# How a routed layer brings its rows to its experts: written to places and read back, or fetched by a list

## The chip, the cores and the metric

The kernel runs on one core of one Trainium2 chip. The metric is device time in microseconds (us), the median of several executions. A second number is the span: the time from the first to the last instruction in an execution that the hardware profiler recorded. Five engines work in parallel on the core, each on its own queue in order: PE (TensorE, matmuls; PEld is its weight load), DVE (VectorE), ACT (ScalarE), POOL (GpSimd) and SP (which issues DMA transfers). They wait for each other through semaphores.

## The reference

Eight layers run one after the other on 625 nodes of 512 features, each adding to `x`: four graph layers and four feed-forward layers. The change lies in the first feed-forward layer, `L0_ffn`: attention over the 625 nodes, a layernorm, and then a routed layer in which each node goes through one of eight experts. Cut to what matters:

```python
t = h.reshape(b * s, d)                       # 625 x 512, after attention and layernorm
probs = softmax(t @ gate_W + gate_b)          # 625 x 8
idx = argmax(probs); gw = max(probs)
hid = gelu(einsum('nd,edf->enf', t, W1) + b1) # eight experts, 512 -> 2048
out_all = einsum('enf,efd->end', hid, W2) + b2
out = einsum('ne,end->nd', one_hot(idx, 8), out_all) * gw[:, None]
```

The output depends only on the chosen expert of each node, so the kernel computes each expert for its own nodes alone.

## The kernel before

The nodes lie as five tiles of 125 rows (`NT = 5`, `P = 125`), the features as four blocks of 128 (`KC = 4`). Each expert has room for 128 nodes (`SLOTS = 128`), so there are 8 x 128 = 1024 places. A node that finds its expert full gets a place beyond these, and a slower path, `L0_late`, computes it; that path runs only if a count, `most`, is over 128, which all engines test at the end of the layer (L891, L892). The trace shows none of its instructions.

The order of the work in `L0_ffn`:

1. SP loads the first six tiles of expert weights, 1 MB each (`ring`, six buffers, L676). It then writes zeros to the 1024 places of `places` (L719) and to part of `made` (L722), both in device memory.
2. Projections and attention; the layernorm of line L164 and L165 leaves the rows in `t_tok`, in the core's memory.
3. The router: `t_tok` transposed (L173), logits `pg` (L230, a helper's line), softmax, the largest of eight, and `oh`, its one-hot.
4. The rank of a node among those of its expert comes from products with a triangle of ones (`before`, L778) and with ones (L779). Expert times 128 plus rank is the node's place: `slot` in f32, `to` as an integer (L791).
5. The rows travel. Five indirect DMAs on POOL (L793) write the 125 rows of each node tile to the places in `places`; eight DMAs on SP (L797) read 128 rows for each expert into `at_e`. All five write the same tensor, and the framework lets each wait for the one before.
6. Meanwhile DVE and PE turn `slot` into a row over all partitions (`srow`, L809 to L812) and make `gt`, the one-hot of the last expert (L828).
7. PE transposes the rows of each expert (L817), DVE and ACT copy them by turns to `xg`.
8. Experts: for each of 8 x 4 steps `first` (16 matmuls, L837), GELU on ACT (L842) and `second` (4 matmuls, L851), one step apart. The rows of experts 0 to 6 go to `made` (L860). In the last expert five indirect DMAs fetch each node's result from `made` (`take`, L866); DVE adds them to `x` (L871). The last expert's own results reach the nodes by a product with `gt` (L875, L889).

A planner decides the order on each engine from dependences and from when a tile's memory comes free. So tiles that are allocated later in the program can be loaded early: the tiles `wx` and `bsel` of the recurrent layer (L1286, L1308) are loaded on ACT's queue at about 519 us, in the middle of `L0_ffn`, and scaled on DVE (L1288, L1309).

Of the kernel before, what the change touches and what calls it, by code (L numbers as in the profile page):

```python
# [15 lines left out]
F32 = mybir.dt.float32  # L16
F16 = mybir.dt.float16
BF16 = mybir.dt.bfloat16
I32 = mybir.dt.int32
U32 = mybir.dt.uint32  # L20
U16 = mybir.dt.uint16
AF = mybir.ActivationFunctionType
ALU = mybir.AluOpType
AX = mybir.AxisListType
# [4 lines left out]
N, D, P, NT = 625, 512, 125, 5  # L29
# [11 lines left out]
SLOTS = 128  # L41
# [608 lines left out]
def L0_ffn(C):  # L650
# [5 lines left out]
    nc, tc, I = C.nc, C.tc, C.ins  # L656
    E8, FF = 8, 2048
# [4 lines left out]
    with ExitStack() as st:  # L662
# [7 lines left out]
        def load(upto):  # L670

            for key in parts[len(loaded):upto]:
# [3 lines left out]
                nc.sync.dma_start(w, src.rearrange("(k p) n -> p k n", p=128))  # L676
                loaded[key] = w


        places = C.dram.tile([E8 * SLOTS + N, D], F32, name="places")  # L680
        made = C.dram.tile([E8 * SLOTS + N, D], F32, name="made")
        zero = pool.tile([128, D], F32, name="zero")
        nc.gpsimd.memset(zero, 0.0)
# [2 lines left out]
        t_tok = pool.tile([P, NT, D], F32, name="t_tok")  # L686
        with ExitStack() as st2:
            apool = st2.enter_context(tc.tile_pool(name="aa", bufs=1))
            qT = apool.tile([128, KC, N], F32, name="qT")
            kT = apool.tile([128, KC, N], F32, name="kT")  # L690
            v = apool.tile([P, NT, D], F32, name="v")
            with tc.tile_pool(name="a_ps", bufs=2, space=PSUM) as ps:
                xT = apool.tile([128, KC, N], F32, name="xT")
                C.feature_major(ps, xT, xn)
                bo = C.row_bcast(pool, W("bo"), D, "bias", 2)
                for t in range(NT):
                    nc.gpsimd.tensor_add(xn[:, t], xn[:, t], bo[:P])
                for dst, w, b in ((qT, "Wq", "bq"), (kT, "Wk", "bk")):
                    wt = C.weight(W(w).rearrange("(k p) n -> p k n", p=128), KC)
                    col = C.columns(pool, ps, W(b).rearrange("(c p) -> c p", p=128), KC, "col_" + b)  # L700
                    for c in range(KC):
                        for n0, n in HALVES:
                            pq = ps.tile([128, 512], F32, name="pq")
                            C.linear_T(pq[:, :n], xT, n0, n, wt, c)
                            nc.scalar.activation(dst[:, c, n0:n0 + n], pq[:, :n], AF.Identity,
                                                 bias=col[:, c:c + 1])
                wt = C.weight(W("Wv").rearrange("(k p) n -> p k n", p=128), KC)
                bv = C.row_bcast(pool, W("bv"), D, "bias", 2)
                for t in range(NT):
                    pv = ps.tile([P, D], F32, name="pv")  # L710
                    C.linear(pv, xT, t, wt)
                    nc.vector.tensor_add(v[:, t], pv, bv[:P])
            wt = C.weight(W("Wo").rearrange("(k p) n -> p k n", p=128), KC)
            g = C.row_bcast(pool, W("ln1_g"), D, "ln_g")
            b = C.row_bcast(pool, W("ln1_b"), D, "ln_b")
            st_ = C.small.tile([P, NT, 6], F32, name="ln_st")

            for e in range(E8):
                nc.sync.dma_start(places[e * SLOTS:(e + 1) * SLOTS], zero[:SLOTS])  # L719
            for r in range((E8 - 1) * SLOTS, E8 * SLOTS + N, 128):  # L720
                n = min(128, E8 * SLOTS + N - r)
                nc.sync.dma_start(made[r:r + n], zero[:n])  # L722

            def finish(t, out):
                for half in range(2):
                    part = xn[:, t, half * 256:(half + 1) * 256]
                    nc.vector.tensor_add(part, part, out[half])
                nc.vector.bn_stats(st_[:, t], xn[:, t])

            C.attention(qT, kT, v, wt, 1.0 / 8.0, False, finish)  # L730
            C.layernorm(t_tok, xn, g, b, st_)

        tT = pool.tile([128, KC, N], F32, name="tT")
        sel = pool.tile([P, NT, E8], F32, name="sel")
# [2 lines left out]
        with ExitStack() as st2:  # L737
            E2 = st2.enter_context
            rpool = E2(tc.tile_pool(name="a_r", bufs=1))
            R = lambda shape, name: rpool.tile(shape, F32, name=name)  # L740
            beyond = R([P, NT], "beyond")
            nc.gpsimd.iota(beyond, pattern=[[P, NT]], base=E8 * SLOTS, channel_multiplier=1,
                           allow_small_or_imprecise_dtypes=True)
            place = R([128, E8], "place")
            nc.gpsimd.iota(place, pattern=[[SLOTS, E8]], base=0, channel_multiplier=1,
                           allow_small_or_imprecise_dtypes=True)
            before = R([P, P], "before")
            nc.vector.tensor_scalar(before, C.iota[:P, :P], place[:P, 0:1], None, op0=ALU.is_gt)
            to = rpool.tile([P, NT], U32, name="to")
            xg = R([128, KC, E8 * SLOTS], "xg")  # L750
            srow = R([128, N], "srow")
            slot, rk, gv = R([P, NT], "slot"), R([P, NT], "rk"), R([P, NT], "gv")
            oh, rank, base = (R([P, NT, E8], k) for k in ("oh", "rank", "base"))
            with tc.tile_pool(name="a_ps3", bufs=2, space=PSUM) as ps, tc.tile_pool(name="a_at", bufs=1) as work:
# [35 lines left out]
                nc.vector.tensor_add(slot, slot, beyond)  # L790
                nc.vector.tensor_copy(to, slot)  # L791
                for t in range(NT):
                    nc.gpsimd.indirect_dma_start(out=places[:, :], in_=t_tok[:, t], in_offset=None,  # L793
                                                 out_offset=bass.IndirectOffsetOnAxis(ap=to[:, t:t + 1], axis=0))
                at_e = [work.tile([SLOTS, D], F32, name="at_e", bufs=E8) for e in range(E8)]
                for e in range(E8):
                    nc.sync.dma_start(at_e[e], places[e * SLOTS:(e + 1) * SLOTS])  # L797
                top = pool.tile([1, 1], F32, name="top")
                nc.vector.tensor_add(base[0:1, 0], base[0:1, NT - 1], pn[0:1, 1, NT - 1])
                nc.vector.reduce_max(top, base[0:1, 0], axis=AX.X)  # L800
# [944 lines left out]


PHASES = [graph_and_L0_gnn, L0_ffn, L1_gnn, L1_ffn, L2_gnn, L2_ffn, L3_gnn, L3_ffn]


# [48 lines left out]
```

## Time and profile before

| what | value |
|---|---|
| median of three runs | 5357.06 us (5355.81 to 5363.99) |
| the profiled execution, its own time | 5365.64 us |
| its span | 5363.8 us, 184920 instructions |
| mean granted TensorE clock | 0.966 |
| PE busy | 4975.2 us, 93% of the span |
| DVE, ACT, POOL busy | 2690.5, 1100.6 and 61.6 us |
| moved by DMA | 232.19 MB, mean 43 GB/s |

The costliest groups of instructions all belong to the recurrent layer, which takes most of the span in 625 steps:

```profile
L1496 PE MATMUL pa<-wp,left 128*23 128x384 bf16 x33312 | 1502.7, 327 | 129.7 <-issue 39.2 <-DVE left L1633 7.4
L1496 PEld LDWEIGHTS pa<-wp,left 128*23 128x23 bf16 x33312 | 811.0, 93 | 643.9 <-DVE left L1633 153.9 <-issue 108.8
```

Such a line gives the kernel's line, the engine and operation, output and inputs with their shapes, and the count; then the busy time in us, the mean duration of one in ns, and the idle time of the engine just before them with what ended it. The routed layer lies between about 455 and 750 us of the span. A timeline line has the start, the busy time, the engine, the line, the operation and its tiles; what stands in brackets is how long the engine had been idle before and what released it. Issuing a DMA isn't counted as busy time, except for indirect DMAs on POOL, which show as instructions[...].

### The profile page before, as it was taken

How to read it: one execution, taken by the hardware profiler on the slowest of the kernel's cores; microseconds unless marked ns; L12 is line 12 of the kernel's file. 1: busy time of each engine (PE TensorE's matmuls, PEld its weight loads, DVE VectorE, ACT ScalarE, POOL GpSimd, SP SyncE). 2: the span in 40 equal slices, each digit the busy share in tenths (PEclk: the TensorE clock that was granted, in tenths of full speed). 3: DMA queues.
4: the chain of work that ended last, by engine and by line, in shares of the span. 5: the costliest groups of instructions: out<-in, count | busy, mean ns of one | idle time of the engine just before them, and what ended most of it. 6: DMA issues, size and time to landing. Idle time of an engine off the chain costs nothing. (4 is left out here: it accounts for less than half of the span.)

```text
span 5363.8 us, 184920 instructions
## 1 busy us (share of the span) xinstructions
PE 4975.2 (93%) x74524; PEld 3140.2 (59%) x74524; DVE 2690.5 (50%) x13552; ACT 1100.6 (21%) x4478; POOL 61.6 (1%) x57
## 2 busy tenths in 40 slices
PE   7986999999999979999999999999999999999988
PEld 5555755555556645555555555565555655555545
DVE  6533024240025146666666656666566666656258
ACT  7433111110115111111111111111111111111125
POOL 0000000000000000000000000000000000000000
PEclk9987998989989989999999999999999999999988
DMA  1031962221116310000000000000000000000100
GB/s 37 34 109 55 319 191 73 89 65 53 45 50 214 124 39 6 7 11 6 6 6 6 6 6 6 6 6 12 7 6 6 6 6 6 6 6 0 54 27 10
DMA packets 167915, 232.19 MB, mean 43 GB/s; under 512 B 64226, under 2 KB 80983, under 8 KB 167000
## 3 DMA queue, kind: packets, MB, share of 16 engines
q1 hardware_dynamic: 155388, 220.04, 12.9%
q10 hardware_dynamic: 10122, 7.55, 0.5%
q0 software_dynamic: 2240, 2.57, 0.2%
q8 instruction: 81, 1.33, 0.1%
q14 instruction: 84, 0.69, 0.0%
HBM read 196.59 MB, written 33.54 MB: 43 GB/s over the span
## 5 line engine op out<-in xcount | busy, mean ns | idle before, releaser
L1496 PE MATMUL pa<-wp,left 128*23 128x384 bf16 x33312 | 1502.7, 327 | 129.7 <-issue 39.2
L1496 PEld LDWEIGHTS pa<-wp,left 128*23 128x23 bf16 x33312 | 811.0, 93 | 643.9 <-DVE left L1633 153.9
L1525 PE MATMUL po<-wo,left 128*1 128x128 f32 x20000 | 659.1, 273 | 0.0
L1525 PEld LDWEIGHTS po<-wo,left 128*1 128x1 f32 x20000 | 482.7, 84 | 126.6 <-issue 0.2
L1537 PE MATMUL spare<-wo,ident 128*128 128x256 f32 x1250 | 437.4, 431 | 25.2 <-issue 25.2
L1611 DVE STREAM_TRANSPOSE col<-pa 128x384 f32<-128x384 f32 x625 | 349.3, 559 | 194.5 <-PE pa L1496 194.5
L1601 DVE COPY col<-gxb 128x16 f32 x625 | 114.4, 183 | 652.0 <-DVEq L1576 652.0
L1568 ACT ACTIVATE act<-ga 128x12 f32<-128x12 f32 x625 | 132.7, 212 | 1185.7 <-DVE ga L1613 1185.7
L1563 ACT COPY xrow<-xsb 1x4 f32<-1x4 f32 x625 | 120.5, 193 | 1211.4 <-ACTq L1561 1211.4
L1537 PEld LDWEIGHTS spare<-wo,ident 128*128 128x128 f32 x1250 | 186.1, 188 | 165.7 <-issue 165.7
L1338 PE MATMUL pg<-xT,w 128*128 128x312 f32 (+1 forms) x1024 | 275.2, 429 | 1.4 <-DVE gt L1347 0.7
L1338 PEld LDWEIGHTS pg<-xT,w 128*128 128x128 f32 x1024 | 193.5, 190 | 82.6 <-DVE gt L1347 4.5
L1488 PE MATMUL lg<-wso,th 128*1 128x8 f32 x5008 | 216.2, 169 | 15.7
L1484 PE MATMUL lg<-wsel,act 128*1 128x8 f32 x5008 | 216.3, 169 | 3.1 <-DVE act L1622 1.2
L1615 DVE STREAM_TRANSPOSE col<-po 128x128 f32<-128x128 f32 x625 | 198.6, 318 | 24.6
L497 PE MATMUL wide<-hot_dst,hot_src 125*125 125x512 bf16 x640 | 178.6, 392 | 27.2 <-DVE hot_dst L477 27.1
L1488 PEld LDWEIGHTS lg<-wso,th 128*1 128x1 f32 x5008 | 147.6, 81 | 74.3 <-DVE wso L1625 12.5
L1481 PEld LDWEIGHTS lg<-xrow,ones 1*1 1x1 f32 x1252 | 51.3, 76 | 237.0 <-issue 237.0
L1625 DVE TENSOR_TENSOR wso<-wsel,so 128x32 f32<-128x32 f32 x625 | 120.2, 192 | 117.2 <-ACT so L1570 112.5
L1484 PEld LDWEIGHTS lg<-wsel,act 128*1 128x1 f32 x5008 | 147.5, 81 | 48.7 <-DVE act L1622 4.6
L230 PE MATMUL po<-w,hT 128*125 128x512 f32 x400 | 175.1, 592 | 0.0
L1570 ACT ACTIVATE so<-go 128x4 f32<-128x4 f32 x625 | 128.2, 205 | 215.3 <-DVE go L1620 215.3
(417 smaller groups left out, 6091.1 us busy)
## 6 DMA issues: line engine op xcount, KB each, us to landing
ring<-in_L_ffn_W_dram SPq DMA_DIRECT2D x64, 1024.0 KB
gxb<-gx SPq DMA_DIRECT2D x25, 800.0 KB
w<-in_L_ffn_WihT_dram SPq DMA_DIRECT2D x16, 1024.0 KB
raw<-in_L_ffn_WhhT_dram SPq DMA_DIRECT2D x24, 512.0 KB
gx<-gt SPq DMA_DIRECT2D x16, 626.0 KB
iw<-gates SPq DMA_DIRECT2D x32, 312.5 KB
gx<-gt SPq DMA_DIRECT2D x16, 624.0 KB
w<-in_L_ffn_W_dram SPq DMA_DIRECT2D x32, 256.0 KB
```

Of the source, the lines that this page charges most:

```text
L230: self.nc.tensor.matmul(out, xT[:, k, t * P:(t + 1) * P], w[:, k, :], start=start and k == 0, stop=stop and k == k_n - 1)
L497: nc.tensor.matmul(wide[i], hs[:, k], hd[:, :W0], start=first, stop=last)
L1338: nc.tensor.matmul(pg[:, :n], w[:, k, s * 128:(s + 1) * 128], xT[:, k, n0:n0 + n], start=k == 0, stop=k == KC - 1)
L1484: pe.matmul(lg, c2[:, s:s + 1], wsel[:, 1, s], start=False, stop=False)
L1488: m = pe.matmul(lg, th[:, s:s + 1], wso[:, s], start=False, stop=s == KC - 1)
L1496: m = pe.matmul(pa[32 * j:32 * j + 2 * GAP + 1], upper[:, s], wp[e][:, s, i, j].rearrange("p g n -> p (g n)"), start=k == 0, stop=k == 11, ...
L1525: m = pe.matmul(po[32 * j:32 * j + 1].rearrange("p (u r) -> p u r", r=32), left[:, s, 0:1], wo[e][:, s].rearrange("p (u j r) -> p j u r", ...
L1537: pe.matmul(spare[:, :256], C.ident, wo[0][:, 0, :256], start=True, stop=True)
L1568: act.activation(act4[:, 0:3].rearrange("p g s -> p (g s)"), ga, AF.Tanh, scale=0.5).then_inc(sem["ifg"])
L1570: act.activation(so, go, AF.Sigmoid).then_inc(sem["so"])
L1611: dve.transpose(col[:, :12, :32], pa.rearrange("p (b r) -> p b r", r=32)).then_inc(sem["ta"])
L1615: dve.transpose(col[:, 12:, :32], po.rearrange("p (s r) -> p s r", r=32)).then_inc(sem["to"])
```

## The change

The rows are no longer written to places. `t_tok` is written as it is, in node order, to a tensor `nodes` in device memory (two DMAs on SP, 112 and 13 partitions). The list of nodes by place is made on the engines: `G` holds, for each node, a one-hot over the 1024 places (five DVE compares of a row of place numbers, `slots`, with `slot`). For each expert PE multiplies its 128 columns of `G` with `ids`, the node's number split in two parts that bf16 holds exactly (a multiple of 256, and the rest). The sum of the two parts is the node in each place, `who`. Eight indirect DMAs on POOL, one for each expert, fetch 128 rows of `nodes` straight into `at_e`. A place that no node has taken holds the number 0 and fetches node 0; its results are never used. The zeroing of `places` goes, that of `made` stays.

```diff
-        places = C.dram.tile([E8 * SLOTS + N, D], F32, name="places")
+        nodes = C.dram.tile([N, D], F32, name="nodes")
@@
-            for e in range(E8):
-                nc.sync.dma_start(places[e * SLOTS:(e + 1) * SLOTS], zero[:SLOTS])
@@
             C.layernorm(t_tok, xn, g, b, st_)
+            for p0, p1 in ((0, 112), (112, P)):
+                nc.sync.dma_start(nodes.rearrange("(t p) d -> p t d", p=P)[p0:p1], t_tok[p0:p1])
@@
+            node, part = R([P, NT], "node"), R([P, NT], "part")
+            ids = rpool.tile([P, NT, 2], BF16, name="ids")
+            nc.gpsimd.iota(node, pattern=[[P, NT]], base=0, channel_multiplier=1,
+                           allow_small_or_imprecise_dtypes=True)
+            nc.vector.tensor_scalar(part, node, 256.0, 256.0, op0=ALU.is_ge, op1=ALU.mult)
+            nc.vector.tensor_copy(ids[:, :, 0], part)
+            nc.vector.tensor_sub(node, node, part)
+            nc.vector.tensor_scalar(part, node, 256.0, 256.0, op0=ALU.is_ge, op1=ALU.mult)
+            nc.vector.tensor_add(ids[:, :, 0], ids[:, :, 0], part)
+            nc.vector.tensor_sub(ids[:, :, 1], node, part)
+            slots = rpool.tile([P, E8 * SLOTS], F16, name="slots")
+            nc.gpsimd.iota(slots, pattern=[[1, E8 * SLOTS]], base=0, channel_multiplier=0,
+                           allow_small_or_imprecise_dtypes=True)
+            G = rpool.tile([P, NT, E8 * SLOTS], BF16, name="G")
+            who_f, who = R([SLOTS, E8], "who_f"), rpool.tile([SLOTS, E8], U32, name="who")
@@
                 for t in range(NT):
-                    nc.gpsimd.indirect_dma_start(out=places[:, :], in_=t_tok[:, t], in_offset=None,
-                                                 out_offset=bass.IndirectOffsetOnAxis(ap=to[:, t:t + 1], axis=0))
+                    nc.vector.tensor_scalar(G[:, t], slots, slot[:, t:t + 1], None, op0=ALU.is_equal)
+                pw = ps.tile([SLOTS, E8, 2], F32, name="pw", bufs=1)
+                for e in range(E8):
+                    for t in range(NT):
+                        nc.tensor.matmul(pw[:, e], G[:, t, e * SLOTS:(e + 1) * SLOTS], ids[:, t], start=t == 0, stop=t == NT - 1)
+                nc.vector.reduce_sum(who_f, pw, axis=AX.X)
+                nc.vector.tensor_copy(who, who_f)
                 at_e = [work.tile([SLOTS, D], F32, name="at_e", bufs=E8) for e in range(E8)]
                 for e in range(E8):
-                    nc.sync.dma_start(at_e[e], places[e * SLOTS:(e + 1) * SLOTS])
+                    nc.gpsimd.indirect_dma_start(out=at_e[e], out_offset=None, in_=nodes[:, :],
+                                                 in_offset=bass.IndirectOffsetOnAxis(ap=who[:, e:e + 1], axis=0))
```

`before`, `node` and `ids` need nothing that the layer computes. On the built program's queues DVE does the six small operations of `ids` among those of the last layernorm; the five compares follow `slot`, PE's 40 products follow the rank products, and the eight gathers stand behind the iotas on POOL's queue. Two small things move with the tiles' memory: the loads of `wx` and `bsel` and a clearing of four columns of the recurrent layer's `xT` now stand at the end of `L0_ffn`, and DVE's scaling of the two in the layernorm of the next layer.

## The prediction

> **What bounds the kernel now.** I read the page first: span 5363.8 us, PE busy 93%. Then I asked for the stages that the change touches, because an average over the span says nothing of them. The view of stages (busy time of each engine, granted clock, share of the DMA engines, GB/s) shows one hole:
>
> ```profile
> core 0: us, PE busy (x) PEld busy (x) DVE busy (x) ACT busy (x) POOL busy (x), PEclk, DMA share, GB/s
> ...
> 455.00:480.00 25.00, 14.01 (x65) 13.23 (x64) 13.74 (x63) 2.88 (x5) 0.00 (x0) 0.54 0.00 1
> 480.00:508.00 28.00, 3.41 (x11) 2.47 (x11) 2.88 (x11) 0.00 (x0) 6.16 (x5) 0.50 0.17 46
> 508.00:519.00 11.00, 7.55 (x32) 6.12 (x32) 2.83 (x5) 2.16 (x4) 0.00 (x0) 0.53 0.55 191
> ...
> 530.00:740.00 210.00, 210.00 (x1201) 152.73 (x1200) 8.60 (x12) 34.30 (x120) 6.53 (x5) 1.00 0.91 306
> ```
>
> From 480 to 508 no engine is busy, and the DMA engines work 17% of the time. From 530 to 740 PE is never idle: the experts' matmuls set the time there, and what comes before them only shifts them. The timeline says what fills the hole:
>
> ```profile
> 479.63 0.17 DVE L791 CAST to<-slot 125x5 uint32<-125x5 f32 x1
> 479.71 0.47 DVE L809 TENSOR_SCALAR junk<-ident,slot 125x125 f32<-125x125 f32 x2
> ...
> 480.13 1.39 POOL L793 DMA_INDIRECT places<-t_tok,to  x1 [26.10 <-DVE junk L809]
> ...
> 485.78 1.20 POOL L793 DMA_INDIRECT places<-t_tok,to  x1 [4.26 <-DMA places<-t_tok,to]
> ...
> 502.24 1.19 POOL L793 DMA_INDIRECT places<-t_tok,to  x1 [4.23 <-DMA places<-t_tok,to]
> 507.53 3.64 SPq L797 DMA_DIRECT2D at_e<-places  x8
> ...
> 510.39 1.94 PE L817 MATMUL pt<-ident,at_e 128*128 128x128 f32 x8 [25.70 <-DMA at_e<-places]
> ...
> 519.24 7.41 PE L837 MATMUL ph<-xg,ring 128*128 128x128 f32 x64 [0.67 <-ACT xg L180]
> ```
>
> Each scatter waits for the one before to land (all five write `places`), and `at_e` waits for the last. So 479.6 (slots known) to 519.24 (first expert matmul) is one chain of 39.6 us: five scatters 5.5 us apart, the reads back, the transposes L817. The view of waits agrees: "PE pt L817 <- DMA at_e<-places" 26.3 us. The same gather form as the new one runs later, with nothing between its issues:
>
> ```profile
> L866 POOL DMA_INDIRECT yt<-made,to x5: 1214/1223/1633, 726.6 to 732.7; - x5
> ...
> DMA to landing us min/median/max: 5.3/5.8/6.0
> ```
>
> Its starts in the timeline are 726.57, 728.11, 729.64, 731.16 and 732.68: 1.53 us apart.
>
> [...]
>
> **The change part by part.**
>
> *Zeroing of places removed* (8 DMAs, 2 MB, SP 291 to 306). Beside it PE runs the q and k projections from 286.94 to 321 without a wait for a DMA. Worth nothing. SP's order behind it is otherwise the same; the load of Wo still stands between blocks of zeroing.
>
> *Write of nodes added* (two DMAs on SP after `t_tok`, about 462). SP has nothing else to do until the ring load at 523, and the DMA share of 455:480 is 0.00. 1.25 MB at the 300 GB/s of the 530:740 row is 4 to 5 us, so it lands near 469, some 19 us before it is read. Nothing.
>
> *Small DVE work added before slots are known.* Six operations on 125x5 (0.17 us each) stand between the last sums of `xn` and the reciprocal, and the compare `before` (0.29 us) moves behind those sums, because POOL's iotas now wait for the last projection matmul (PE ends at 455.2) and no longer for the last L330 (453.7). Some of it fills waits of the chain. I take +1.0 us (0.5 to 1.6). POOL's new iota of 1024 columns costs about 1.1 us (L81: 625 columns, 0.65 us) and has 20 us to spare.
>
> *One-hot G* (five, 125x1024 bf16 from f16). Nearest rows: L477, 125x625 with the same types, 386 ns, and L470, 125x125, 253 ns: 0.27 ns a column. 1024 columns then take 0.49 us, and start 0.41 us apart: 4 x 0.41 + 0.49 = 2.1 us. If the type path fell to that of L828 (128x625 f32, 0.54 us) it would be 4.4 us.
>
> *Product pw* (40 matmuls, weights 128 columns bf16, two columns moving). Four go while G is made; 36 follow. PE's clock is 0.5 here. The logits L230 (125 columns f32) take 5.05 us for 24, 0.21 us each[...]. 36 x 0.105 + 0.3 to start and drain = 4.1 us (2.2 to 7.9).
>
> *who_f, who.* 0.2 us each, but the order puts a copy of `srow` between, which waits for its PE product behind the 40: 1.3 us. Then POOL starts 0.3 us after (as from 479.80 to 480.13).
>
> So the first gather starts at 479.7 + 1.0 + 2.1 + 4.1 + 1.3 + 0.3 = 488.5, 8.4 us later than the first scatter. DVE's copies of `srow` and the compare `gt` behind these were done at 485.5 and now end near 492, still before rows land.
>
> *Gathers* (eight of 128 rows in place of five scatters and eight reads). No wait stands between them; each has its own tile. Seven steps of 1.53 us: the last starts at 499.2. Landing: 5.2 us is the scatter's[...]. I take the middle, 4.2, with 3.2 and 5.8 as ends: 503.4. Then the last expert's transposes and copy, about 1.6 us (517.65 to 519.24 in before): **505.0** in place of 519.24, **14.2 us** less.
>
> *What is late next.* PE transposes an expert in 0.95 us, less than 1.53, so POOL's issue is what ends last. After 505.0 PE is the bound: six weight tiles lie ready, and the experts need 306 GB/s whether they start early or late.
>
> *Moved by the allocator.* The loads `wx` and `bsel` of the later recurrent layer and a memset go from about 519 to the end of this layer: ACT issues them after the last scatter matmul (about 749 in before's time), and DVE scales them (2 x 0.18 us) in the next layernorm, between L154 and L156 (754.3). Loaded at 749.1 plus the 3.3 us they took before (519.74 to 523.02), they are there by 752.4. I take +0.3 us; behind DVE's scaling waits ACT's root at 754.92 and with it PE at 759. If they landed 2 us late, it would cost 2.
>
> **Sum:** 14.2 - 0.3 = 13.9 us. The profiled execution took 5365.64 us (span 5363.8) and would take 5351.7; the median shown, 5357.06, is 8.6 us below it, with the three runs from 5355.81 to 5363.99, so I forecast 5357.06 - 13.9 = 5343.2 us.
>
> **Rivals.** 0.2% is 10.7 us, about what a measurement of this kernel can tell from no change.
> 1. *The place list costs its dear ends*: G 2.3 us more, pw 3.8 us more, landing 1.6 us more, 7.7 us in all, leaves 6.2 us: 5350.9. [...] Against: the rows L477 and L866. 0.16.
> 2. *Slower: the gathers do not overlap.* If they land 5.5 us apart as the scatters do, seven steps cost 38.5 in place of 10.7, and the first expert matmul comes at 532.8: 13.9 us lost, 5371. It turns to a loss from 3.5 us a gather on (13.9 / 7 over 1.53). A reason to fear it: of 1024 places only 625 are taken, so 399 rows read node 0, one address, and eight gathers stand in the queue where five have been seen. Against: L866's 1.53 us, and the load of `bo`, 128 reads of one row, which was there 5.4 us after its issue (279.60 to POOL's start at 285.07) while the ring loads ran. 0.08.
> 3. *The gain is given back elsewhere*: the moved loads land late, or the recurrent loop's 625 steps shift with the program's new layout. Nothing in the order shows a change there. 0.10, at about 5352.
>
> **How the numbers follow.** The forecast has 0.66, its own range 5336 (POOL at its busy 1.22 us per gather, landing 3.2, cheap pw and DVE work: 2.2 + 1.0 + 1.9 + 0.5 = 5.6 less, and a little run spread) to 5349. Rivals 1 and 3 take the range to 5355 and leave the loss outside, with some of the third. Faster by over 0.2% means under 5346.3: nine tenths of the forecast and a third of rivals 1 and 3, 0.68. Slower: rival 2 and a bad case of 3, 0.10. The rest, 0.22, lies within.
>
> **What would show it.** Right: eight POOL issues from about 488 at 1.2 to 1.6 us; PE's transposes of `at_e` (L817 before, L838 after) spaced by landings, the last near 503; the first expert matmul near 505; 530:740 as full as before, 14 us earlier. Wrong: gathers landing over 3.5 us apart, 40 `pw` pairs over 6 us, G at 0.9 us each, or DVE waiting at L1309 (L1288 before) for `wx`.

## The result, and the profile after

The changed kernel took 5342.83 us, median of 9 runs (5335.22 to 5347.84), and the kernel before 5362.66 us on the same chip (9 runs, 5355.81 to 5374.44). The ratio is 0.9959, 95% interval 0.995 to 0.9968: faster by 0.3 to 0.5%. The profiled execution has a span of 5338.5 us, against 5363.8 before.

The view of stages of the changed kernel, cut at the cast of `to`, at the first expert matmul, and in the experts (columns as before):

```profile
455.00:479.00 24.00, 13.83 (x64) 13.23 (x64) 12.76 (x67) 2.88 (x5) 0.27 (x1) 0.51 0.17 54
479.00:498.00 19.00, 12.62 (x84) 8.88 (x84) 8.32 (x24) 2.34 (x4) 7.79 (x8) 0.59 0.36 110
498.00:508.00 10.00, 10.00 (x65) 9.87 (x66) 0.00 (x0) 2.55 (x6) 0.00 (x0) 0.74 0.45 131
520.00:720.00 200.00, 200.00 (x1142) 145.27 (x1141) 8.60 (x12) 33.13 (x116) 5.99 (x5) 1.00 0.90 307
```

The 28 us in which little worked (PE for 3.4 of them) are gone: 19.0 us stand where 39.6 stood, and POOL is busy for 7.8 of them. In the experts nothing changed: PE never idle, 307 GB/s. But the third line shows a stage that wasn't there before: PE is busy all the time, at a mean clock of 0.74. The timeline of the changed kernel:

```profile
478.98 0.17 DVE L806 CAST to<-slot 125x5 uint32<-125x5 f32 x1
479.06 2.06 DVE L808 TENSOR_SCALAR G<-slots,slot 125x1024 bf16<-125x1024 f16 x5
...
481.19 1.12 PE L812 MATMUL pw<-ids,G 125*128 125x2 bf16 x36 [0.21 <-DVE G L808]
...
482.34 0.17 DVE L813 TENSOR_REDUCE who_f<-pw 128x8 f32<-128x16 f32 x1 [0.83 <-PE pw L812]
...
483.18 0.16 DVE L814 CAST who<-who_f 128x8 uint32<-128x8 f32 x1
...
483.63 1.17 POOL L817 DMA_INDIRECT at_e<-nodes,who  x1 [28.36 <-DVE who L814]
...
485.10 0.96 POOL L817 DMA_INDIRECT at_e<-nodes,who  x1 [0.30 <-issue]
...
492.61 0.94 POOL L817 DMA_INDIRECT at_e<-nodes,who  x1 [0.30 <-issue]
...
496.26 1.05 PE L838 MATMUL pt<-ident,at_e 128*128 128x128 f32 x4 [0.45 <-DMA at_e<-nodes,who]
...
497.99 9.85 PE L858 MATMUL ph<-xg,ring 128*128 128x128 f32 x64 [0.68 <-ACT xg L180]
```

Read it as a sum. From `to` to the first gather 4.65 us; seven steps to the last gather 8.98 us; from there until PE begins on its rows 3.65 us; transposes and copy 1.73 us: 19.01 us. The brackets at POOL say "issue", no longer "DMA places": no gather waits for another. The view of the tile `at_e` gives the rest of the price:

```profile
L817 POOL DMA_INDIRECT at_e<-nodes,who x8: 942/946/1165, 483.6 to 492.6; - x8
...
DMA to landing us min/median/max: 3.4/3.6/3.8
```

The last line of the timeline carries the first thing that was lost again: the first 64 expert matmuls take 9.85 us; before they took 7.41. These 64 are the first two of the 32 steps: the trace has 32 records for the 16 matmuls of a step, two for each f32 matmul that isn't a transpose (the logits have 40 records for 20, while the 40 products of `pw` in bf16 have 40). The granted clock (third column from the right) says why they are slower. First the kernel before around its first expert matmul at 519.24, then the changed kernel around its own at 497.99:

```profile
516.00:518.00 2.00, 2.00 (x10) 1.64 (x9) 0.79 (x2) 0.59 (x1) 0.00 (x0) 0.50 0.00 0
518.00:520.00 2.00, 1.33 (x10) 1.06 (x9) 0.63 (x2) 0.59 (x1) 0.00 (x0) 0.93 0.03 7
520.00:522.00 2.00, 2.00 (x20) 2.00 (x19) 0.00 (x0) 0.00 (x0) 0.00 (x0) 1.00 0.78 233
```

```profile
494.00:496.00 2.00, 1.09 (x8) 0.65 (x7) 0.16 (x2) 0.58 (x1) 0.00 (x0) 1.00 0.51 166
496.00:498.00 2.00, 1.06 (x5) 0.69 (x5) 0.55 (x1) 0.58 (x1) 0.00 (x0) 0.58 0.00 0
498.00:500.00 2.00, 2.00 (x9) 2.00 (x10) 0.00 (x0) 0.00 (x0) 0.00 (x0) 0.50 0.56 118
500.00:502.00 2.00, 2.00 (x12) 2.00 (x11) 0.00 (x0) 0.00 (x0) 0.00 (x0) 0.50 0.42 153
502.00:504.00 2.00, 2.00 (x15) 2.00 (x15) 0.00 (x0) 0.00 (x0) 0.00 (x0) 0.71 0.00 0
504.00:506.00 2.00, 2.00 (x20) 2.00 (x19) 0.00 (x0) 1.65 (x3) 0.00 (x0) 1.00 0.36 26
```

Before, the rows were all there, PE transposed with hardly a pause, and the clock was up at 518.3, a us before the experts. Now the rows come 1.25 us apart and PE works half of the time. The clock rises at 492.9, is back at 0.50 at 496.3, and rises again only at 503.1, 5 us after the experts' start. a_warm below tries this cause.

The second loss stands at the layer's end. In the kernel before the last sum (L889) ends at 749.84 and the next layer's first normalized rows (L161) start at 758.15, 8.31 us later. In the changed kernel L910 ends at 731.03 and L161 starts at 740.10, 9.07 us later. Its timeline there:

```profile
730.33 0.34 ACTq L1307 DMA_DIRECT2D wx<-in_L_ffn_WselT_dram  x1
730.69 0.46 ACTq L1329 DMA_DIRECT2D bsel<-in_L_ffn_b_sel_dram  x1
...
735.50 0.15 DVE L1309 TENSOR_SCALAR wx<-wx 128x32 f32<-128x32 f32 x1
735.56 0.16 DVE L1330 TENSOR_SCALAR bsel<-bsel 128x4 f32<-128x4 f32 x1
...
735.71 0.35 ACTq L98 DMA_DIRECT2D bias<-in_L_gnn_b_dram  x1
...
737.16 1.28 ACT L119 ACT_TABLE_LOAD   x1 [17.88 <-issue]
```

DVE waits for nothing here; `wx` and `bsel` are there in time. It is ACT that is late: the loads of three rows stand on its queue before the table load, and they go out only from 735.71 on (in the kernel before at 751.67, 1.83 us after its last sum; here 4.68 us after). What holds them is the test of `most` at the layer's end. It stands on ACT's queue behind the loads of `wx` and `bsel`, and the queue goes on 3.2 us after it. View of the test's line on ACT, first of the kernel before (L892), then of the changed one (L913):

```profile
L892 ACTq COMPARE_BRANCH  x1: 50/50/50, 746.5 to 746.5; - x1
L892 ACTq EVENT_SEMAPHORE  x1: 17/17/17, 749.7 to 749.7; - x1
```

```profile
L913 ACTq COMPARE_BRANCH  x1: 50/50/50, 732.1 to 732.1; - x1
L913 ACTq EVENT_SEMAPHORE  x1: 17/17/17, 735.3 to 735.3; - x1
```

Before, the test came 3.4 us ahead of the last sum, and its 3.2 us lay beside the sums; now it comes 1.0 us behind them.

So the balance up to L161 is 20.60 us (39.61 less 19.01) - 2.44 - 0.76 + 0.65 = 18.05 us, and 758.15 - 740.10 is 18.05. The 0.65 is what `to` comes earlier; as 0.69 us stand already at the layer's first normalized rows (279.55 and 278.86), it doesn't come from the change. What the change gives at L161 is therefore 17.40 us.

### The profile page after: what moved, and what is told of

Its sections match the earlier page's. It is cut to its first block, busy times and chain, and to the rows that moved or that the text cites. A ratio compares the mean times of both kernels' runs of the same rounds, so it can differ in the third digit from the quotient of the medians.

```text
span 5338.5 us, 185001 instructions
## 1 busy us (share of the span) xinstructions
PE 4975.0 (93%) x74564; PEld 3129.1 (59%) x74564; DVE 2689.9 (50%) x13565; ACT 1099.3 (21%) x4478; POOL 63.5 (1%) x62
## 3 DMA queue, kind: packets, MB, share of 16 engines
q0 software_dynamic: 1760, 3.38, 0.2%
## 5 line engine op out<-in xcount | busy, mean ns | idle before, releaser
L1517 PEld LDWEIGHTS pa<-wp,left 128*23 128x23 bf16 x33312 | 797.8, 93 | 650.0 <-DVE left L1654 152.3
```

The costliest lines, as they stand in the source:

```text
L1517: m = pe.matmul(pa[32 * j:32 * j + 2 * GAP + 1], upper[:, s], wp[e][:, s, i, j].rearrange("p g n -> p (g n)"), start=k == 0, stop=k == 11, ...
```

## The experiments

To compare the kernels without what the other layers do, I take three stretches from each trace: from the cast of `to` to the first expert matmul; the duration of the first experts' matmuls; and from `to` to L161 of the next layer. The column "rest" is the span behind L161, a part that no edit touches. The first matmuls are 64 records (two steps) or, where transposes follow the first step, 32; the first 32 take 3.84 us in the kernel before and 6.28 in the changed one. The diffs show the lines that carry the change.

| kernel | `to` to first `ph` | first `ph` matmuls | `to` to L161 | rest | device time, runs |
|---|---|---|---|---|---|
| before | 39.61 | 64: 7.41 | 278.52 | 4605.7 | 5362.66, 9 |
| changed | 19.01 | 64: 9.85 | 261.12 | 4598.4 | 5342.83, 9 |
| b_five_tensors | 21.95 | 64: 7.41 | 260.04 | 4615.7 | 5356.27, 1 |
| a_two_buffers | 27.07 | 64: 9.23 | 268.75 | 4595.9 | 5344.67, 1 |
| a_rows_125 | 23.41 | 64: 9.88 | 265.69 | 4600.1 | 5350.56, 1 |
| a_spread_rows | 19.24 | 64: 9.85 | 261.73 | 4613.4 | 5357.57, 1 |
| a_warm | 20.20 | 64: 7.41 | 260.05 | 4603.0 | 5345.11, 1 |
| a_short_lists | 19.44 | 64: 9.90 | 259.24 | 4602.6 | 5341.02, 1 |
| a_zeroed | 19.02 | 64: 9.82 | 261.25 | 4600.0 | 5341.49, 1 |
| a_early_experts | 10.77 | 32: 5.61 | 255.39 | 4606.4 | 5340.80, 5 |
| a_again | 19.37 | 64: 9.62 | 261.34 | 4601.5 | 5343.54, 6 |
| c_early_lists | 10.82 | 32: 5.63 | 253.35 | 4612.1 | 5345.31, 8 |
| c_early_warm | 10.57 | 32: 6.20 | 254.01 | 4609.1 | 5340.74, 6 |
| c_early_warm2 | 10.39 | 32: 3.84 | 251.51 | 4607.2 | 5337.00, 4 |

The rest varies by 20 us over the traces; between the two traces of the changed kernel (changed, a_again) it differs by 3.1 us. A single device time therefore says little about an edit worth a few us; the three stretches do.

**Was it the waiting? (b_five_tensors)** The kernel before, with one tensor of places for each node tile; each expert reads one of the five, so rows of the other tiles are left out.

```diff
-        places = C.dram.tile([E8 * SLOTS + N, D], F32, name="places")
+        places = [C.dram.tile([E8 * SLOTS + N, D], F32, name=f"places{t}") for t in range(NT)]
@@
-                nc.sync.dma_start(places[e * SLOTS:(e + 1) * SLOTS], zero[:SLOTS])
+                nc.sync.dma_start(places[e % NT][e * SLOTS:(e + 1) * SLOTS], zero[:SLOTS])
@@
-                    nc.gpsimd.indirect_dma_start(out=places[:, :], in_=t_tok[:, t], in_offset=None,
+                    nc.gpsimd.indirect_dma_start(out=places[t][:, :], in_=t_tok[:, t], in_offset=None,
@@
-                    nc.sync.dma_start(at_e[e], places[e * SLOTS:(e + 1) * SLOTS])
+                    nc.sync.dma_start(at_e[e], places[e % NT][e * SLOTS:(e + 1) * SLOTS])
```

> The kernel before, with each of the five scatters writing a tensor of its own, so that none waits for another; each expert reads from one of them, so it gets the rows of one node tile only. Measure: from the slots known (start of the cast `to`) to the first expert matmul, 39.6 us before and 19.0 us after the change. If waiting on one another is what the five scatters cost: they start 1.2 to 1.5 us apart, land about 5.2 us after that, the last near 11 us after the slots, and the stage is about 23.5 us. If a scatter of 125 rows itself holds the queue[...] for 5 us: landings stay near 5 us apart and the stage is 36 us or more.

Timeline of b_five_tensors:

```profile
478.62 0.17 DVE L791 CAST to<-slot 125x5 uint32<-125x5 f32 x1
...
479.12 1.39 POOL L793 DMA_INDIRECT places<-t_tok,to  x1 [26.08 <-DVE junk L809]
...
480.81 1.19 POOL L793 DMA_INDIRECT places<-t_tok,to  x1 [0.30 <-issue]
...
485.30 1.19 POOL L793 DMA_INDIRECT places<-t_tok,to  x1 [0.30 <-issue]
...
500.57 7.41 PE L837 MATMUL ph<-xg,ring 128*128 128x128 f32 x64 [0.67 <-ACT xg L180]
```

Without the common tensor the stage falls from 39.61 to 21.95 us: 17.66 of the 20.60 us. Starts are 1.5 us apart in place of 5.5, and the last one comes 6.68 us after `to` and no longer 22.61: that is 15.93 us.

The other 1.7 us are no proof for the waiting: each read here waits for one scatter alone, so the first reads go out at 484.7, before the last scatter has even started. A kernel with right rows couldn't do that. Its stage can be estimated: 6.68 us, plus the 17.00 that the kernel before takes from its last scatter to its first expert matmul, plus up to 1.1 because these scatters land in 6.3 us and not in 5.2; 23.7 to 24.8 us in all. So the wait of each write for the one before is worth 14.8 to 15.9 us of the stage's 20.60, about three quarters, and the list has the remaining 4.7 to 5.8. At L161 this kernel is even with the changed one (260.04 and 261.12), because its clock is up (7.41) and its `wx` is early.

**Does the gathers' own buffering matter? (a_two_buffers)**

```diff
-                at_e = [work.tile([SLOTS, D], F32, name="at_e", bufs=E8) for e in range(E8)]
+                at_e = [work.tile([SLOTS, D], F32, name="at_e", bufs=2) for e in range(E8)]
```

> The changed kernel with two tiles for the gathered rows in place of eight, so that gather e waits for the transposes of expert e-2. If the gain lives on gathers that overlap: two gathers per 5.3 us (3.6 landing, transposes 1.1, and the waits on both sides), the stage from slots to the first expert matmul grows from 19.0 to 25 to 28 us. If POOL's issue at 1.25 us a gather were enough to explain the pace, with the landing not seen: 19 to 20 us.

The gathers now start at 482.54, 484.00, 487.66, 489.23, 492.95, 494.51, 497.92 and 499.40, every second one from the third on released by "PE pt L838" after 2.5 to 2.8 us of idle time on POOL. The stage takes 27.07 us: a gather that has to wait for its buffer brings the old chain back, and eight buffers are worth 8 us.

**128 rows or 125? (a_rows_125)** Each gather fetches 125 rows; the last three places of each expert are zero, from a clearing of `xg` ahead of the layer's router, and the transposes take 125 rows.

```diff
-                    nc.gpsimd.indirect_dma_start(out=at_e[e], out_offset=None, in_=nodes[:, :],
-                                                 in_offset=bass.IndirectOffsetOnAxis(ap=who[:, e:e + 1], axis=0))
+                    nc.gpsimd.indirect_dma_start(out=at_e[e][:P], out_offset=None, in_=nodes[:, :],
+                                                 in_offset=bass.IndirectOffsetOnAxis(ap=who[:P, e:e + 1], axis=0))
```

> The changed kernel with gathers of 125 rows in place of 128; the last three places of each expert stay zero. If the short landing (3.6 us, where 5.2 was measured for the scatters) comes from 128 rows[...]: landing goes back to 5 us or more, the stage from 19.0 to about 20.5 us. If it comes from reading in place of writing device memory: landing stays at 3.6 us, the stage at 19.0.

View of the tile `at_e` in a_rows_125:

```profile
L818 POOL DMA_INDIRECT at_e<-nodes,who x8: 1210/1212/1390, 487.6 to 498.4; - x8
...
DMA to landing us min/median/max: 5.7/5.8/6.2
```

Three rows fewer cost 2.2 us of landing (5.8 against 3.6) and 0.27 us of POOL for each (1.212 against 0.946); the stage grows by 4.4 us, where the expectation, which counted the landing alone, had 1.5. The packets differ too: POOL's queue has 2240 in the kernel before, whose ten transfers all move 125 rows, and 1760 in the changed kernel, with eight transfers of 128 rows and five of 125. That is 224 packets for 125 rows and 80 for 128. The longer landing and POOL's longer time go with more packets, but no third number of rows was tried, so what sets them is open.

**Does the one row cost that 399 free places read? (a_spread_rows)** The list is replaced by one with different nodes in all places of an expert; the experts then work on rows that aren't theirs.

```diff
+            spread = R([SLOTS, E8], "spread")
+            nc.gpsimd.iota(spread, pattern=[[71, E8]], base=0, channel_multiplier=1,
+                           allow_small_or_imprecise_dtypes=True)
@@
-                nc.vector.tensor_copy(who, who_f)
+                nc.vector.scalar_tensor_tensor(who, who_f, 0.0, spread, op0=ALU.mult, op1=ALU.add)
```

> The changed kernel with the list replaced, after it is made, by different rows in all places of an expert (node 71 e + p), so that no row is read twice in a gather; the experts get other rows than the router chose. If the 399 free places that all fetch node 0 cost nothing: landing 3.5 to 3.7 us and the stage 19.0 us, as in the changed kernel. If reading one row some 50 times in a gather slows it: landing under 3.3 us.

Landing 3.3/3.6/3.8 us against 3.4/3.6/3.8, POOL 0.947 against 0.946 us, the stage 19.24 against 19.01. Reading one row 399 times costs nothing that can be seen.

**Is the slow start of the experts the clock? (a_warm)** The transposes of experts 3 to 7 are done a second time, into a tile that nothing reads, so that PE has fewer pauses.

```diff
+                    if e >= 3:
+                        for k in range(KC):
+                            nc.tensor.transpose(warm[:, k * SLOTS:(k + 1) * SLOTS], at_e[e][:, k * 128:(k + 1) * 128], C.ident[:SLOTS, :SLOTS])
```

> The changed kernel with the transposes of experts 3 to 7 done twice, the second time into a spare tile, so that PE has no pauses while the last gathers land. In the changed kernel the first two expert steps took 9.85 us where 7.41 us were seen before, and from the slots known to the first matmul of the second layer 28.7 us pass. If PE's clock, still halved after the pauses between gathers, is the reason: the two steps take 7.4 to 8.0 us and the stretch 26 to 27 us, with the first expert matmul where it was (19.0 us, at most 0.7 later). If weights or something else hold the first steps: 9.8 us and 28.7 us as before.

View of stages of a_warm:

```profile
494.00:496.00 2.00, 2.00 (x11) 2.00 (x10) 0.00 (x0) 0.59 (x1) 0.42 (x1) 0.50 0.63 184
496.00:498.00 2.00, 2.00 (x15) 2.00 (x14) 0.69 (x1) 0.36 (x1) 0.00 (x0) 0.66 0.20 80
498.00:500.00 2.00, 1.78 (x17) 1.54 (x15) 0.69 (x1) 0.81 (x2) 0.00 (x0) 1.00 0.00 0
```

Busy without a pause from 493.2, PE has its full clock from 497.4, and the 64 matmuls take 7.41 us, as before. The added work delays their start by 1.19 us (20.20 against 19.01), so 1.25 us are left: the first `y` comes 27.45 us after `to` and not 28.70, and 261.12 becomes 260.05. More work on PE made the layer shorter.

**Is the loss at the layer's end the place of `wx`? (a_short_lists)** `slots` and `G` go to the pool that is closed ahead of the experts, so the planner has the old addresses again.

```diff
-            slots = rpool.tile([P, E8 * SLOTS], F16, name="slots")
-            G = rpool.tile([P, NT, E8 * SLOTS], BF16, name="G")
+                slots = work.tile([P, E8 * SLOTS], F16, name="slots")
+                G = work.tile([P, NT, E8 * SLOTS], BF16, name="G")
```

> The changed kernel with the tiles slots and G in the pool of the gathered rows, which closes before the experts, so that the planner puts the loads wx and bsel back to where the gathers end. From the end of the last sum of this layer to the first normalised tile of the next: 8.3 us before, 9.1 us after the change. If the moved loads cost this: 8.3 us. If it has another reason: 9.1 us. The stage from slots to the first expert matmul stays 19.0 us either way.

`wx` is loaded at 497.0 again, and the stretch from the last sum to L161 is 6.70 us (729.53 to 736.23), not 9.07. Timeline of a_short_lists:

```profile
730.90 0.34 ACTq L98 DMA_DIRECT2D bias<-in_L_gnn_b_dram  x1
...
733.17 1.28 ACT L119 ACT_TABLE_LOAD   x1 [15.39 <-DVE ln_st L152]
```

The table load starts 3.64 us after the last sum; in the changed kernel it was 6.13. The stretch is also 1.6 us shorter than the 8.31 us of the kernel before, which has `wx` early as well. There ACT's three loads were issued from 751.67 to 754.89, here from 730.90 to 733.14; why they took 3.2 us there and 2.2 here is open. Over all 14 traces the stretch takes 6.70 to 8.31 us where `wx` is loaded early (six traces) and 9.07 to 9.44 where it is late (eight), without overlap. The kernel before is the slowest of the early ones and the changed kernel the fastest of the late ones, so 0.76 us is the smallest difference between the two places.

**Was the zeroing really free? (a_zeroed)** The tensor `places` and its eight writes of zeros are put back.

```diff
+        places = C.dram.tile([E8 * SLOTS + N, D], F32, name="places")
@@
+            for e in range(E8):
+                nc.sync.dma_start(places[e * SLOTS:(e + 1) * SLOTS], zero[:SLOTS])
```

> The changed kernel with the eight writes of zeros that it dropped put back, to a tensor that nobody reads. If dropping them is worth nothing, as forecast: from the first normalised tile of this layer to the slots known the same as in the changed kernel within 0.3 us, and the stage after it 19.0 us. If the 2 MB held up something in the attention stage: 1 us or more longer.

From the layer's first L161 to `to`: 199.98 us with the zeroing (278.10 to 478.08), 200.12 in the changed kernel, 200.08 in the kernel before. It costs nothing.

**Must all experts' rows be there first? (a_early_experts)** Only the first expert is transposed ahead of the experts; the other seven, one in each of the first steps, into the PSUM banks of `acc`, which are free until the end. For that the pool of `at_e` stays open, and `slots` and `G` get a pool of their own; `wx` stays late (722.59).

```diff
-                for e in range(E8):
+                for e in range(1):
@@
+            def turn(e):
+                pt = acc[e % NT]
+                for k in range(KC):
+                    nc.tensor.transpose(pt[:, k * SLOTS:(k + 1) * SLOTS], at_e[e][:, k * 128:(k + 1) * 128], C.ident[:SLOTS, :SLOTS])
+                C.copy(e, xg[:, :, e * SLOTS:(e + 1) * SLOTS], pt.rearrange("p (k n) -> p k n", k=KC))
@@
                 first(e, q)
+                if 1 <= i + 1 < E8:
+                    turn(i + 1)
```

> The changed kernel with only the first expert's rows turned before the experts begin; the others are turned one per step, into PSUM banks that are free until the end, so that the experts start when the first gather has landed and not the last. If the landing of the last gather is what the experts wait for: slots to the first expert matmul 10 to 11 us in place of 19.0; the seven transposes then lie in PE's time, about 3 us, so the layer ends 4 to 7 us earlier, about 0.1% of the time. If the weights' loads then bound the experts: PE waits inside the expert stage and the layer's end moves by under 2 us.

The first expert matmul comes 10.77 us after `to` and L161 5.73 us earlier than in the changed kernel (255.39 against 261.12). Of the 8.24 us at the start, the seven transposes inside the steps take back part: a step with one lasts 7.45 us (508.63 to 516.08), one without 7.01 (509.61 to 516.62 in a_short_lists). The clock is still at 0.5 at the start: the first step's 32 matmuls take 5.61 us, the second step's 3.74. The device time, 5340.80 us (ratio to before 0.9949, interval 0.9935 to 0.9963), can't be told from the changed kernel's.

**The changed kernel again, and two combinations (a_again, c_early_lists, c_early_warm).** a_again has no edit. c_early_lists is a_early_experts with the pool of `at_e` at the other end of the on-chip memory, so that `wx` and `bsel` are early. c_early_warm adds fifteen transposes that read only the identity.

```diff
-            work = E2(tc.tile_pool(name="a_at", bufs=1))
+            work = E2(tc.tile_pool(name="a_at", bufs=1, side="right"))
@@
+                    for k in range(3):
+                        nc.tensor.transpose(warm[:, k * 128:(k + 1) * 128], C.ident, C.ident)
```

> The changed kernel once more, unaltered, beside the two combinations. If the rest of the program behind the layer only varies by itself, the stage from the cast of `to` to the first expert matmul is 19.0 us again and the time from the cast to the next layer's first normalized rows 261.1 us again, while the time from there to the end of the span may lie anywhere between 4596 and 4616 us, where the ten executions seen so far lie. If the change itself shortens the rest, that time is within 2 us of the 4598.4 us of its first trace.

> First expert early, with the eight tiles of fetched rows at the other end of the on-chip memory, so that wx and bsel are loaded early again. If the 5.7 us of the early first expert and the 2.4 us of the early loads are separate, the time from the cast of `to` to the next layer's first normalized rows is 255.4 - 2.4 = 253.0 us (261.1 in the changed kernel), with a first expert of 5.6 us and about 6.7 us between the last sum and the normalized rows; the device time is 8 us under the changed kernel's, ratio 0.9985 between the two. If the loads' place doesn't matter, 255.4 us.

> The same, with fifteen transposes of the identity into a spare PSUM tile put between the matmuls for srow, while the first rows are on their way. If the tensor engine's clock rises after some 4 us of unbroken work, it is at 1.00 when the first expert starts, whose 32 matmuls take 3.7 instead of 5.6 us, and the time from the cast to the next layer's normalized rows falls by another 1.9 us to about 251 us. If the pauses for DVE between the srow matmuls keep it at 0.5, the first expert still takes 5.6 us; if the added transposes hold up the first rows' transposes, the first expert matmul starts later than 10.8 us after the cast.

a_again repeats the layer (261.34 us) and has another rest, 4601.5 us. c_early_lists gives 253.35 us where 253.0 was expected: the two gains add up. But its device time, 5345.31 us, median of 8, is no better than the 5343.54 of a_again, measured beside it, where 8 us less was expected. In the profiled execution, which is near the median (5345.61), its rest is 4612.1 us, 10.6 more than in a_again. So it isn't shown that the rest is independent of the edit. Most of the 10.6 us can be located: the first matmul of `acc` from `hid` in the next layer (L1121 in the changed kernel) comes 104.4 us after L161 in a_again and 108.5 in c_early_lists. The stages between, from 66 us after L161 in both, first of a_again and then of c_early_lists:

```profile
805.52:811.52 6.00, 6.00 (x41) 5.67 (x40) 3.47 (x20) 1.16 (x2) 0.00 (x0) 0.68 0.00 0
811.52:817.52 6.00, 6.00 (x36) 5.92 (x36) 1.29 (x7) 0.00 (x0) 0.00 (x0) 0.61 0.01 3
```

```profile
797.75:803.75 6.00, 6.00 (x30) 5.67 (x30) 3.30 (x13) 1.16 (x2) 0.00 (x0) 0.50 0.00 0
803.75:809.75 6.00, 6.00 (x31) 6.00 (x30) 1.81 (x11) 0.00 (x0) 0.00 (x0) 0.50 0.01 3
```

The same matmuls, PE busy for all of both, and 41 + 36 of them done in one against 30 + 31 in the other: the clock rose for a while in a_again (at 1.00 from 809.4 to 812.8) and didn't in c_early_lists. The 14 traces fall in two groups at this matmul: ten at 104.1 to 104.8 us, and b_five_tensors, a_warm, c_early_lists and c_early_warm at 108.3 to 108.7. Of the first group, the kernel before, the changed kernel and a_again have such a stretch at full clock; of the second, b_five_tensors, like c_early_lists, has none (0.50 from 798.7 to 822.7). The recurrent loop adds its own: from the first to the last of its matmuls pa (L1496 before) it is 3083.9 to 3099.0 us, 3085.2 in a_again and 3089.4 in c_early_lists. What makes the loop differ is open.

c_early_warm didn't try what it was to try. The tile view puts its transposes at 453.3 to 454.9 us: reading nothing but a constant, they were ordered 25 us too early. The first step took 6.20 us.

**Warm-up at the right place (c_early_warm2).** The added transposes read the diagonal `dg` that the matmul for `srow` reads, so they can't run before it.

```diff
+                    for k in range(4):
+                        nc.tensor.transpose(warm[:P, k * P:(k + 1) * P], dg, C.ident[:P, :P])
```

> In c_early_warm the fifteen transposes read only the identity and ran at 453 us, 25 us too early. Here four transposes for each tile of nodes read the diagonal that the matmul for srow reads, so they can't start before it: twenty transposes lie between 479 and 486 us after the start, in the wait for the first rows. If about 4 us of little-interrupted work raise the clock, the first expert's 32 matmuls take 3.7 us (5.6 in c_early_lists) or a part between, and the time from the cast of `to` to the next layer's first normalized rows is 251.5 us (253.35 in c_early_lists). If the clock stays at 0.5, the first expert takes 5.6 us and the time is 253.3 to 254.5 us.

View of stages of c_early_warm2; the rows of the first expert arrive at 486:

```profile
480.00:482.00 2.00, 2.00 (x25) 2.00 (x22) 0.60 (x4) 0.00 (x0) 0.24 (x1) 0.50 0.15 41
482.00:484.00 2.00, 2.00 (x11) 2.00 (x11) 1.09 (x4) 0.00 (x0) 1.70 (x2) 0.50 0.88 238
484.00:486.00 2.00, 2.00 (x16) 1.95 (x14) 0.87 (x3) 0.00 (x0) 1.39 (x3) 0.75 0.73 227
486.00:488.00 2.00, 1.18 (x10) 0.92 (x9) 1.44 (x3) 0.00 (x0) 1.63 (x2) 1.00 0.60 199
```

In c_early_lists, whose `to` is 1.3 us later, the stages from 482 to 490 have PE busy for 0.8 to 1.4 of 2 us and a clock of 0.50 throughout. Here the clock is up at 485, the first 32 matmuls take 3.84 us, and the layer 251.51 us, 9.6 us less than in the changed kernel. The device time is 5337.00 us, median of 4 (5334.39 to 5337.68), ratio to before 0.9943, interval 0.9927 to 0.996. It is the lowest of all, but the interval of a_again, 0.9953 to 0.9978, overlaps it, and the two weren't run side by side: that it beats the changed kernel end to end is likely and not shown.

## Why the prediction was right, and where its numbers were off

The forecast was 5343.2 us, the measured median 5342.83. The mechanism is the one it named. That the number agrees to 0.4 us is luck: two errors of nearly 6 us cancel.

- *What bounds*: right. The scatters' wait for one another was most of the hole: without it (b_five_tensors) the last scatter starts 15.93 us sooner. The prediction says that no engine is busy in the 28 us; its own line has POOL busy for 6.2 of them and PE for 3.4.
- *Zeroing and the write of nodes*: nothing, as said. For the zeroing a_zeroed shows it. The write of `nodes` was issued at 461.2 and 461.5; the DMA share is 0.98 in 462:464 and 0.01 again in 468:470, and the first gather, at 483.63, waited for `who`.
- *Small DVE work*, +1.0: from attention's last L335 to `to` it is 26.56 against 25.92 us, +0.64; over the whole stretch from L161 to `to` only 0.04 of it is left. In a_short_lists, where POOL's iotas come sooner and the six operations stand in DVE's waits, it is 25.92 again, so the operations themselves cost nothing.
- *G*, 2.1: measured 2.06.
- *pw*, 4.1: measured 1.1. This is the term that was mis-sized most. The 0.105 us that it takes for each of the 36 is half the 0.21 us of a logit record; the half was the author's estimate and isn't shown by a trace. Nor was 0.21 us the time of a whole product: the trace has two records for each of the logits' 20 products. Measured, 36 pairs of load and product went by in 1.12 us, 31 ns each, at a clock of 0.50, though a single load's record lasts 104 ns. Why these loads are so quick wasn't tried.
- *who_f, who*: 1.3 and 0.3, measured 1.0 (482.34 to 483.34) and 0.29.
- *Gathers*: 1.53 us apart, measured 1.25; landing 4.2, measured 3.6. The row that stood for them, L866, moves 125 rows. a_rows_125 has both of its numbers again, 1.51 us apart and 5.8 us to landing; the prediction let the number of rows change the landing and not POOL's time. The lower end of its landing, 3.2 us, was the author's estimate and isn't shown by the trace of before. Seven steps make it 1.7 us too much (10.7 against 8.98).
- *What is late next*: POOL's issue, as said. What was not said is that rows which come one by one leave PE with pauses, and that this has a price, 2.44 us in the first two steps. The prediction has no term for the clock at the experts' start.
- *wx and bsel*, +0.3: measured +0.76, and by another way. The prediction watched DVE's scaling, which waited for nothing; the price is on ACT's queue, where the test of `most` comes behind the two loads and the three loads of the next layer go out later.
- *The sum*: 13.9 us forecast; 17.40 at the next layer (18.05 with the 0.65 that were there before), and 19.8 between the two medians. Where the other 2.4 arise isn't shown; the rest of the span varies by more. The error at the next layer came mostly from pw (3.0), the gathers' spacing (1.7), the DVE work (1.0) and the landing (0.4), less the two losses. The number met because the starting point, 5357.06 from three runs, lay 5.6 us under the 5362.66 of nine.
- *Rivals*: the dear ends of the place list didn't come; the gathers overlap (1.25 us apart, against 3.5 from which it would have been a loss), and the row read by all free places is no hindrance; a give-back elsewhere exists, of 3.2 us, while the recurrent loop differs by up to 15 us between the 14 traces, for reasons that no run tells.

## What to carry to other kernels

When indirect writes into one tensor stand behind one another at a landing's distance (here 5.5 us), look at that wait first: here it was worth 14.8 to 15.9 us of a stage of 39.6. A tensor for each write takes it away, but the rows then have to be put together from five tensors, which b_five_tensors leaves out and nobody built; the list does without. Price a gather by a row with the same number of partitions: here 128 rows took 22% less of POOL's time than 125 (0.946 us against 1.212) and landed 38% sooner (3.6 us against 5.8). When a wait goes and data begin to arrive piece by piece, look at the granted clock of what comes next (here 0.50 for the first 5 us of the experts), and start the consumer with the first piece: that shortened this layer by 5.7 us, though the device time doesn't show it yet.

## What was not expected of the hardware

- PE's busy time alone didn't tell whether the clock rose. In the changed kernel the logits keep PE busy for 10 us without a pause (462 to 472), mostly in weight loads with eight columns moving, and the clock stays at 0.50:

```profile
464.00:466.00 2.00, 2.00 (x11) 2.00 (x11) 0.00 (x0) 1.11 (x1) 0.00 (x0) 0.50 0.95 313
466.00:468.00 2.00, 2.00 (x12) 2.00 (x12) 0.67 (x1) 0.00 (x0) 0.00 (x0) 0.50 0.14 35
```

  In unbroken work that was mostly transposes with 125 or 128 columns the clock was up after 4.1 us (a_warm, 493.2 to 497.4) and 4.7 us (c_early_warm2, 480.3 to 485.0). In the changed kernel it is up for 3.4 us (492.9 to 496.3) and down for 6.8 (to 503.1). The short rise in the next layer, with which 4 us less go there, lasts 3.4 us as well: 828.9 to 832.3 in the kernel before, 810.3 to 813.8 in the changed kernel, 809.4 to 812.8 in a_again. Why unbroken work raised it in these two runs and not in the logits no run here tells.
- POOL's time for an indirect DMA: 0.946 us for 128 rows and 1.212 for 125, with 0.30 us between two in both (a_rows_125), and 80 packets against 224.
- The part of the program that no edit touches took 4595.9 to 4615.7 us over 14 traces, more than the whole change is worth. The stretch from `to` to L161 was repeatable to 0.3 us: 261.12 and 261.34 in two traces of the changed kernel, 261.25 in a_zeroed. Its parts differed by up to 0.4 us (19.01 and 19.37 to the first expert matmul).
